# Starting the second expert layer on the first ten strips' rows while the last strips are still being routed

## The chip, the core and the metric

The kernel runs on one core of a Trainium2 chip. The metric is the device time of one execution in microseconds (us); for the kernel before, three runs were timed. A profile of one further execution on the same chip type gives the durations used below. Engines are TensorE (PE, with its weight loads as PEld), VectorE (DVE), ScalarE (ACT), GpSimd (POOL) and SyncE (SP); SP issues most of the plain loads and stores, GpSimd the indirect ones.

## What is computed

Two layers, each with a token mixer (windowed attention in layer 0, two ternary 3x3 convolutions with batch norm in layer 1) and a mixture of experts with 8 experts, of which each token uses 2. There are 2 x 56 x 56 = 6272 tokens of 256 channels. The part that the change touches is the experts of layer 1:

```python
def _L1_ffn_ref(x, gate_w, gate_b, W1, b1, W2, b2):
    ...
    logits = xf @ gate_w + gate_b
    probs = jax.nn.softmax(logits, axis=-1)
    top2_vals, top2_idx = jax.lax.top_k(probs, 2)
    cw = jnp.zeros((N, Ee), dtype=xf.dtype).at[jnp.arange(N)[:, None], top2_idx].add(top2_vals)

    def step(acc, params):
        w1, bb1, w2, bb2, we = params
        h = jax.nn.gelu(xf @ w1 + bb1, approximate=False)
        y = h @ w2 + bb2
        return (acc + we[:, None] * y, None)
...
x = x + _L1_conv_ref(_ln_c(x), ...)
t = _to_tokens(x)
t = t + _L1_ffn_ref(_ln_t(t), ...)
```

The hidden width of an expert is 512 in layer 1 and 256 in layer 0. The kernel computes only the two chosen experts of each token.

## The kernel before

**Tiling.** The image is cut into 14 strips of 8 rows, 448 tokens each, and a strip into 4 blocks of 112 tokens (`TT`). Experts work on tiles of `G` = 256 rows of one expert. Whatever the router says, `NTILE` = 56 tiles hold all 12544 token-expert pairs.

**Routing layer 1** (`routing`, L724, driven by `in_order`, L1816). For each strip, `residual` (L1783) loads the strip's tokens as they were ahead of the convolutions (`back`, two buffers, L1789, on SP's queue), finishes the batch norm and adds both (L1792, L1795, L1804, L1808). `norm` (L743) makes the normalised rows `u` (six buffers) and the logits (L758 to L781). `in_order` interleaves strips: a strip is begun in one turn of its loop, and its addition L1808 comes a turn later. `settle` (L786) takes a batch of strips (`BATCHES`, the last ones in pairs), finds the two best experts of each token and the row of each pair in its expert's part of the array `xs` in HBM. Then it issues, on GpSimd's queue, one indirect DMA for each block and choice that scatters 112 rows to `xs` (L854): 8 for a strip, 112 in all. The row's place depends on the tokens ahead of it, so that places grow from strip to strip.

**Planning.** After all strips, `tiles(1)` (L885) computes on VectorE, from the counts of rows of each expert, which expert and which first row each tile has (`where`), and `gates` (L867) the weights of the sums. `tiles` can also be called for a part: `tiles(0)` plans those tiles that are certain to be full after the first `FIRST[layer]` strips, and `tiles(1, taken)` the others. Layer 0 does this with `FIRST[0]` = 10 and so `EARLY[0]` = 27 early tiles. Layer 1 has `FIRST[1]` = 0, so that all 56 tiles are planned at the end and read their rows after all scatters.

**Experts** (`experts`, L982, and `experts_in_order`, L988). The order is written out by hand. For each tile, `fetch_weights` (L1012) reads the expert's number into a register of SP and loads 1.15 MB of weights (four buffers, three tiles ahead); `fetch_rows` (L999) reads the first row and loads 256 rows (six buffers, four ahead). `turn` (L1019) transposes the rows on TensorE and copies them on ScalarE (L1025, L1029), `first` (L1047) is the first product with its gelu (L1056, L1063), and `second` (L1065) the second product, the bias on VectorE (L1080, five buffers of y) and two scatters to `ys` on GpSimd's queue (L1082).

**Order.** `manual_schedule` keeps the order of the Python text on SP, VectorE, TensorE and ScalarE. All instructions of an engine, and the loads of SP's queue, are issued in that order, and an instruction that waits holds up those behind it. Dependencies between DMAs that touch the same array are taken as real unless two groups are declared apart: `disjoint` (L633) and `apart` (L639). Pools are stacks in SBUF: a pool that is opened where another was closed waits for that one's users.

**The last stage** (L1859 on) gathers each token's two rows from `ys`, adds them with the gates' weights, and writes the output.

Of the kernel before, what the change touches and what calls it, by code (L numbers as in the profile page):

```python
# [13 lines left out]
I32 = mybir.dt.int32  # L14
# [3 lines left out]
PSUM = bass.MemoryType.PSUM  # L18
# [42 lines left out]
TAPS = 9  # L61
COMPS = 4
DEN = HEADS * NT // TT
FIRST = (10, 0)

EARLY = tuple(max(0, (TOP * NT * n - E * (G - 1)) // G) for n in FIRST)
ROWS_AHEAD, AHEAD = 4, 3
# [559 lines left out]
def metaformer(ctx: ExitStack, tc: tile.TileContext, a: dict, out: bass.AP, flag):  # L627
# [354 lines left out]
    def experts(layer, FF, plans, ys, wp, tp, ps, at_tile=None):  # L982


        with tc.manual_schedule(engines=ENGINES):
            experts_in_order(layer, FF, plans, ys, wp, tp, ps, at_tile)

    def experts_in_order(layer, FF, plans, ys, wp, tp, ps, at_tile):  # L988
        NF = FF // P
        GP = G // P  # L990
        wts = a[f"L{layer}_experts"]
# [7 lines left out]
        def fetch_rows(j):  # L999
            where, _, _, n = planned(j)  # L1000
            r = nc.sync.value_load(
                where[0:1, 1, n : n + 1], min_val=0, max_val=E * ROWS - G
            )
            xg = tp.tile([P, GP, RW], F32, tag="xg", name="xg", bufs=6)
            o = nc.sync.dma_start(
                xg, xs[bass.ds(r, G), :].rearrange("(p i) c -> p i c", i=GP)
            )
            if j < EARLY[layer]:
                disjoint(o, f"early{layer}", f"late{layer}")
            live.setdefault(j, {})["xg"] = xg  # L1010

        def fetch_weights(j):  # L1012
# [79 lines left out]
        for j in range(AHEAD):  # L1092
            live[j] = {}
            fetch_weights(j)
        for j in range(ROWS_AHEAD):
            fetch_rows(j)
        turn(0)
# [2 lines left out]
        for j in range(NTILE):  # L1100
            if j + ROWS_AHEAD < NTILE:
                fetch_rows(j + ROWS_AHEAD)
            if j + AHEAD < NTILE:
                fetch_weights(j + AHEAD)
            if j + 2 < NTILE:
                turn(j + 2)
            if j + 1 < NTILE:
                first(j + 1)
            second(j)
            if at_tile is not None:  # L1110
                at_tile(j)

    def gather(i, ys, wgt, tp, xt, bufs):

# [140 lines left out]
    with ExitStack() as st:  # L1255
# [322 lines left out]
        x_all = None  # L1578
        X, XT, pad, sums = {}, {}, [], []
        mid = ctx.enter_context(ExitStack())  # L1580
        wq_held = ExitStack()

        def routed_all():

            nonlocal x_all
            plans0.append(tiles0(1, *taken))
            gates0()
            unfit = aw.tile([TT, 1], F32, tag="unfit", name="unfit")
            nc.vector.tensor_scalar(fits, fits, float(len(STRIPS)), None, ALU.is_lt)
            nc.vector.tensor_reduce(unfit, fits, AX.X, ALU.add)  # L1590
            unfit_b = aw.tile([TT, 1], BF16, tag="unfit_b", name="unfit_b")
            nc.vector.tensor_copy(unfit_b, unfit)
            pf = ps.tile([P, 1], F32, tag="aux", name="pf")
# [12 lines left out]
            cp = mid.enter_context(tc.tile_pool(name="pads", bufs=1, reuse_waits="tile"))  # L1606
            for b in range(B):
                t = cp.tile([P, KC, HC, WC], F32, tag=f"pad{b}", name=f"pad{b}")
                nc.gpsimd.memset(t[:, :, 0:1, :], 0.0)
                nc.gpsimd.memset(t[:, :, HC - 1 : HC, :], 0.0)  # L1610
                nc.gpsimd.memset(t[:, :, 1 : HC - 1, 0:1], 0.0)
                nc.gpsimd.memset(t[:, :, 1 : HC - 1, WC - 1 : WC], 0.0)
                pad.append(t)
            mid.enter_context(wq_held)
            wqp = wq_held.enter_context(tc.tile_pool(name="wq", bufs=1, reuse_waits="tile"))

            some = x_all[:, len(STRIPS) - 3 :].rearrange("p s c -> p (s c)").bitcast(BF16)
            sums.append(some.rearrange("p (k n c) -> p k n c", k=KC, n=COMPS))
            sums.append(wqp.tile([P, KC, COMPS, 3 * C], BF16, tag="sums", name="sums"))
# [23 lines left out]
    with mid:  # L1643
# [130 lines left out]
            scale2, shift2 = affine(stats, bn["g2"], bn["b2"], rt)  # L1774
        wq_held.close()

        wp1 = mid.enter_context(tc.tile_pool(name="moe_w1", bufs=4, reuse_waits="tile"))
        with ExitStack() as st:
            wp = st.enter_context(tc.tile_pool(name="route_w1", bufs=1, reuse_waits="tile"))
            tp = st.enter_context(tc.tile_pool(name="route_t1", bufs=2, reuse_waits="tile"))  # L1780
            ps = st.enter_context(tc.tile_pool(name="route_ps1", bufs=2, space=PSUM, reuse_waits="tile"))

            def residual(i):  # L1783

# [26 lines left out]
                yield from residual(i)  # L1811
                yield from norm(i, XT[STRIPS[i]][:TT])

            norm, settle, tiles, gates, wgt1, _ = routing(1, wp, tp, ps)

            def in_order():  # L1816

# [4 lines left out]
                for i in range(n + 2):  # L1822
                    young, old = i - 1, i - 2
                    if young in jobs:
                        next(jobs[young])
                    finish(ready)
                    if young == 0:
                        next(jobs[young])
                    if i < n:
                        jobs[i] = strip(i)  # L1830
                        next(jobs[i])
                    if young > 0 and young in jobs:
                        next(jobs[young])
# [155 lines left out]
```

## Time and profile before

| what | value |
|---|---|
| time, median of 3 runs | 1845.31 us (1836.94 to 1851.86) |
| profiled execution, its own time | 1841.35 us |
| its span, first to last instruction | 1839.5 us |
| TensorE busy | 1560.3 us, 85% |
| VectorE, ScalarE, GpSimd busy | 51%, 39%, 37% |
| routing of layer 1, about | 1178 to 1323 us |
| experts of layer 1, about | 1356 to 1770 us |
| gathering and output | the last 69 us |

Times within the profile count from the span's start. On a row of the timeline the first number is the start, the second how long it took (or, where rows were merged, x3 for example, from the first start to the last end), then engine, line, operation, and what is written from what, with the shape. In square brackets is how long the engine stood idle ahead of it and what ended the wait. The `SPq` rows are the issuing of DMAs on SP's queue, not their transfer.

### The profile page before, as it was taken

What the parts mean: (1) busy time and instruction counts of PE and PEld (TensorE: products, weight loads), DVE (VectorE), ACT (ScalarE), POOL (GpSimd) and SP (SyncE); (2) the same over time, 40 slices, a digit from 0 to 9 for tenths busy, and PEclk for the clock granted to TensorE, in tenths of its full rate; (3) what the DMA queues carried; (4) which work ended last, traced back from release to release, by engine and by line L of the source; (5) the groups of instructions that cost most, each with busy time, mean ns of one, the idle gap of its engine ahead of it and who ended that gap; (6) DMA issues with size and microseconds to landing.
All of it is one profiled execution on the core that took longest, in us unless ns stands there. A gap on an engine that the chain in (4) does not pass through costs nothing. (4 is left out here: it accounts for less than half of the span.)

```text
span 1839.5 us, 25711 instructions
## 1 busy us (share of the span) xinstructions
PE 1560.3 (85%) x8649; PEld 1233.4 (67%) x8649; DVE 934.5 (51%) x2618; ACT 709.1 (39%) x1347; POOL 677.6 (37%) x682
## 2 busy tenths in 40 slices
PE   6999997998768969866889899788359999999964
PEld 3555564555457857754778788677348888888852
DVE  3457657465625367847886555587501111111137
ACT  3454443343323434536553622255223333333312
POOL 3012544424423764442454143067732222222210
PEclk9999999999878989987999899855569999999975
DMA  8022333212257977866441000044446666666648
GB/s 246 21 83 83 112 101 114 72 45 80 83 159 228 302 276 247 303 208 194 145 144 31 0 1 1 21 121 134 164 141 229 237 237 225 228 234 234 216 150 308
DMA packets 89742, 283.23 MB, mean 154 GB/s; under 512 B 20391, under 2 KB 32763, under 8 KB 79297
## 3 DMA queue, kind: packets, MB, share of 16 engines
q1 hardware_dynamic: 64288, 223.25, 38.3%
q0 software_dynamic: 21504, 51.82, 8.0%
q10 hardware_dynamic: 3808, 6.42, 1.0%
q8 instruction: 70, 1.15, 0.3%
q14 instruction: 72, 0.58, 0.1%
HBM read 209.98 MB, written 75.12 MB: 155 GB/s over the span
## 5 line engine op out<-in xcount | busy, mean ns | idle before, releaser
L1056 PE MATMUL ph<-ut,w 128*128 128x256 f32 x1344 | 322.6, 391 | 5.5 <-DMA w<-in_L_experts 5.3
L1072 PE MATMUL py<-w,h 128*128 128x256 f32 x1344 | 310.3, 381 | 0.0
L1082 POOL DMA_INDIRECT ys<-y,to x170 | 170.7, 1004 | 370.9 <-DVE dest L1032 282.6
L1080 DVE TENSOR_TENSOR y<-py,w 128x512 f32<-128x512 f32 x112 | 77.4, 691 | 436.0 <-PE py L1072 318.9
L1072 PEld LDWEIGHTS py<-w,h 128*128 128x128 f32 x1344 | 257.7, 192 | 36.0
L1056 PEld LDWEIGHTS ph<-ut,w 128*128 128x128 f32 x1344 | 255.5, 197 | 39.1 <-DMA w<-in_L_experts 6.9
L1714 PE MATMUL pc<-hi,wq 128*128 128x448 f32 x672 | 256.8, 383 | 17.8 <-ACT hi L1685 17.8
L854 POOL DMA_INDIRECT xs<-u,pos x224 | 217.4, 971 | 127.7 <-issue 61.6
L1714 PE MATMUL pc<-lo,wq 128*128 128x448 f32 x672 | 255.8, 381 | 0.0
L1063 ACT ACTIVATE h<-ph,w 128x256 f32<-128x256 f32 x336 | 158.2, 474 | 123.7 <-PE ph L1056 123.2
L1416 ACT ACTIVATE ex<-sc 112x476 f32<-112x476 f32 (+3 forms) x224 | 116.3, 571 | 208.9 <-PE sc L1406 207.9
L1029 ACT COPY ut<-pt 128x512 f32<-128x512 f32 x112 | 65.5, 585 | 313.5 <-PE pt L1025 313.5
L1684 POOL TENSOR_TENSOR v<-pad 128x928 f32<-128x928 f32 (+1 forms) x56 | 98.3, 1762 | 162.6 <-DVE lo L1686 152.6
L1714 PEld LDWEIGHTS pc<-hi,wq 128*128 128x128 f32 x672 | 129.5, 193 | 33.1 <-ACT hi L1685 19.1
L1714 PEld LDWEIGHTS pc<-lo,wq 128*128 128x128 f32 x672 | 129.9, 193 | 15.1 <-DVE lo L1686 0.7
L1426 PE MATMUL av<-ex,vals 112*64 112x238 f32 (+3 forms) x896 | 121.2, 391 | 19.0 <-DVE acc L1436 18.8
L1025 PE MATMUL pt<-ident,xg 128*128 128x128 f32 x448 | 71.3, 284 | 60.6 <-DMA xg<-xs 57.7
L1436 DVE TENSOR_TENSOR acc<-av,acc 128x238 f32<-128x238 f32 (+3 forms) x224 | 87.3, 407 | 66.1 <-PE av L1426 64.0
L1025 PEld LDWEIGHTS pt<-ident,xg 128*128 128x128 f32 x448 | 57.6, 147 | 85.0 <-DMA xg<-xs 58.5
L1426 PEld LDWEIGHTS av<-ex,vals 112*64 112x64 f32 x896 | 55.6, 139 | 66.8 <-DVE acc L1436 24.8
L1685 ACT CAST hi<-v 128x928 fp32r<-128x928 f32 x56 | 54.1, 966 | 114.0 <-PE pc L1714 107.2
L1397 PE MATMUL sc<-q_im,keys 32*112 32x238 f32 (+3 forms) x896 | 89.7, 418 | 2.0 <-ACT ex L1416 1.9
(233 smaller groups left out, 2206.5 us busy)
## 6 DMA issues: line engine op xcount, KB each, us to landing
w<-in_L_experts SPq DMA_DIRECT2D x56, 1154.0 KB
w<-in_L_experts SPq DMA_DIRECT2D x56, 641.0 KB
xg<-xs SPq DMA_DIRECT2D x112, 260.0 KB
got<-ys SPq DMA_DIRECT2D x28, 896.0 KB
acc<-in_fresh SPq DMA_DIRECT2D x14, 896.0 KB
xt<-in_x_tok SPq DMA_DIRECT2D x14, 448.0 KB
xr<-in_x_tok SPq DMA_DIRECT2D x14, 448.0 KB
rec<-shares SPq DMA_DIRECT2D x28, 224.0 KB
```

What stands on the lines that cost most here:

```text
L854: w = nc.gpsimd.indirect_dma_start(xs[:, :], bass.IndirectOffsetOnAxis(ap=pos[:, j, t0 + t : t0 + t + 1], axis=0), us[t // NTT][:, t % NTT ...
L1025: nc.tensor.transpose(pt[:, k, i * P : (i + 1) * P], d["xg"][:, i, k * P : (k + 1) * P], ident)
L1056: nc.tensor.matmul(ph[:, :G], w1[:, k, f * P : (f + 1) * P], d["ut"][:, k, :], start=k == 0, stop=k == KC - 1,)
L1063: nc.scalar.activation(d["h"][:, f, :], ph[:, :G], AF.Gelu, bias=b1[:, f : f + 1])
L1072: nc.tensor.matmul(py[:, i, :], d["h"][:, f, i * P : (i + 1) * P], w2[:, f, :], start=f == 0, stop=f == NF - 1,)
L1082: o = nc.gpsimd.indirect_dma_start(ys[:, :], bass.IndirectOffsetOnAxis(ap=d["to"][:, i : i + 1], axis=0), y[:, i, :], None, bounds_check=T ...
L1397: nc.tensor.matmul(sc[h // 2][:, h % 2, :nq], keys[g][p, c, tx * TT : (tx + 1) * TT], q_im[p, c, r0:r1, c0:c1], start=True, stop=False,)
L1416: nc.scalar.activation(e[:, :, :nq], sc[j][:, :, :nq], AF.Exp, scale=HD**-0.5)
L1426: nc.tensor.matmul(av[VW * i : VW * (i + 1), :nq], vals[g % 3][:, tx, 2 * c + j, 2 * i : 2 * i + 2, :].rearrange("p a d -> p (a d)"), ex[j ...
L1436: nc.vector.tensor_tensor(d, av[:, :nq].rearrange("p (h w) -> p h w", w=c1 - c0), d, ALU.add)
L1684: (nc.gpsimd if u else nc.vector).tensor_tensor(v[:, :, at : at + n, :], *r, op)
L1714: nc.tensor.matmul(pc[:, :NT], wq[:, k, c, dx * C + o * P : dx * C + (o + 1) * P], part[:, k, :, dx : dx + W], start=m == 0, stop=m == 2 * ...
```

## The change

Layer 1 now also plans in two parts: 27 tiles from the first ten strips, the other 29 at the end. The experts' driver becomes a generator in three steps. The first step, which loads the weights of the first three tiles, is run inside the routing loop, as soon as strip 9 has been settled (which is in the turn that begins strip 12, ahead of that strip's first instructions). A load of one element of `xs` on GpSimd's queue (`fence`) follows there. After planning and gates, SP reads the loaded element, and then the experts go on; their early tiles' row loads are declared apart from all of layer 1's scatters. The pools for weights and routing move to the right side of SBUF, and the pads of the convolution are closed when routing is over, so that the tiles' buffers can be opened there.

```diff
-FIRST = (10, 0)
+FIRST = (10, 10)
...
         with tc.manual_schedule(engines=ENGINES):
-            experts_in_order(layer, FF, plans, ys, wp, tp, ps, at_tile)
-
-    def experts_in_order(layer, FF, plans, ys, wp, tp, ps, at_tile):
+            steps = experts_in_order(layer, FF, plans, ys, wp, at_tile)
+            next(steps)
+            steps.send((tp, ps))
+
+    def experts_in_order(layer, FF, plans, ys, wp, at_tile):
...
             if j < EARLY[layer]:
-                disjoint(o, f"early{layer}", f"late{layer}")
+                disjoint(o, f"early{layer}", f"rows{layer}" if layer else f"late{layer}")
...
         for j in range(AHEAD):
             live[j] = {}
             fetch_weights(j)
+        tp, ps = yield
         for j in range(ROWS_AHEAD):
             fetch_rows(j)
...
+        yield
...
-            cp = mid.enter_context(tc.tile_pool(name="pads", bufs=1, reuse_waits="tile"))
+            cp = pads.enter_context(tc.tile_pool(name="pads", bufs=1, reuse_waits="tile"))
...
-        wp1 = mid.enter_context(tc.tile_pool(name="moe_w1", bufs=4, reuse_waits="tile"))
-        with ExitStack() as st:
-            wp = st.enter_context(tc.tile_pool(name="route_w1", bufs=1, reuse_waits="tile"))
-            tp = st.enter_context(tc.tile_pool(name="route_t1", bufs=2, reuse_waits="tile"))
-            ps = st.enter_context(tc.tile_pool(name="route_ps1", bufs=2, space=PSUM, reuse_waits="tile"))
+        with ExitStack() as both:
+            wp1 = both.enter_context(
+                tc.tile_pool(name="moe_w1", bufs=4, side="right", reuse_waits="tile")
+            )
...
-            norm, settle, tiles, gates, wgt1, _ = routing(1, wp, tp, ps)
+            norm, settle, tiles, gates, wgt1, sent = routing(1, wp, tp, ps)
+
+            def fence():
+
+                some = wp.tile([1, 1], I32, tag="some", name="some")
+                nc.gpsimd.dma_start(some, xs[0:1, 0:1].bitcast(I32))
+                fences.append(some)
...
                     finish(ready)
+                    if not plans1 and FIRST[1] - 1 in sent:
+                        plan, n_early = tiles(0)
+                        plans1.append(plan)
+                        next(experts1)
+                        fence()
                     if young == 0:
...
                 finish(ready)
-
+                return n_early
+
+            plans1, fences = [], []
+            experts1 = experts_in_order(1, 2 * C, plans1, ys[1], wp1, None)
             with tc.manual_schedule(engines=ENGINES):
-                in_order()
-                plans1 = [None, tiles(1)]
+                plans1.append(tiles(1, in_order()))
                 gates()
 
-        with ExitStack() as st:
-            tp = st.enter_context(tc.tile_pool(name="moe_t1", bufs=2, reuse_waits="tile"))
-            ps = st.enter_context(tc.tile_pool(name="moe_ps1", bufs=2, space=PSUM, reuse_waits="tile"))
-            experts(1, 2 * C, plans1, ys[1], wp1, tp, ps)
+                nc.sync.value_load(fences[0])
+
+                route_ps.close()
+                pads.close()
+                tp1 = both.enter_context(tc.tile_pool(name="moe_t1", bufs=2, reuse_waits="tile"))
+                ps1 = both.enter_context(
+                    tc.tile_pool(name="moe_ps1", bufs=2, space=PSUM, reuse_waits="tile")
+                )
+                experts1.send((tp1, ps1))
```

`side="right"` stands on `route_w1` and `route_t1` as well.

More of the change, by code (lines that the diff above doesn't have):

```diff
@@ L1580, in metaformer @@
         mid = ctx.enter_context(ExitStack())
+        pads = mid.enter_context(ExitStack())
         wq_held = ExitStack()
@@ L1775, in metaformer @@
         wq_held.close()
-        wp1 = mid.enter_context(tc.tile_pool(name="moe_w1", bufs=4, reuse_waits="tile"))
-        with ExitStack() as st:
-            wp = st.enter_context(tc.tile_pool(name="route_w1", bufs=1, reuse_waits="tile"))
-            tp = st.enter_context(tc.tile_pool(name="route_t1", bufs=2, reuse_waits="tile"))
-            ps = st.enter_context(tc.tile_pool(name="route_ps1", bufs=2, space=PSUM, reuse_waits="tile"))
+        with ExitStack() as both:
+            wp1 = both.enter_context(
+                tc.tile_pool(name="moe_w1", bufs=4, side="right", reuse_waits="tile")
+            )
+            wp = both.enter_context(
+                tc.tile_pool(name="route_w1", bufs=1, side="right", reuse_waits="tile")
+            )
+            tp = both.enter_context(
+                tc.tile_pool(name="route_t1", bufs=2, side="right", reuse_waits="tile")
+            )
+            route_ps = ExitStack()
+            ps = route_ps.enter_context(
+                tc.tile_pool(name="route_ps1", bufs=2, space=PSUM, reuse_waits="tile")
+            )
             def residual(i):
@@ L1847, in in_order @@
                 finish(ready)
+                return n_early
+            plans1, fences = [], []
+            experts1 = experts_in_order(1, 2 * C, plans1, ys[1], wp1, None)
             with tc.manual_schedule(engines=ENGINES):
-                in_order()
-                plans1 = [None, tiles(1)]
+                plans1.append(tiles(1, in_order()))
                 gates()
-        with ExitStack() as st:
-            tp = st.enter_context(tc.tile_pool(name="moe_t1", bufs=2, reuse_waits="tile"))
-            ps = st.enter_context(tc.tile_pool(name="moe_ps1", bufs=2, space=PSUM, reuse_waits="tile"))
-            experts(1, 2 * C, plans1, ys[1], wp1, tp, ps)
+                nc.sync.value_load(fences[0])
[4 more added lines that the diff above has]
+                    tc.tile_pool(name="moe_ps1", bufs=2, space=PSUM, reuse_waits="tile")
+                )
+                experts1.send((tp1, ps1))
     with ExitStack() as st:
```

## The prediction

> **What bounds the kernel now.** I looked first at the forty slices: TensorE falls to 3 and then 5 tenths in slices 28 and 29, between the second convolution and the last long run of nines, and the granted clock is 5 tenths there. The chain of waits, read in order of time, has that place as scatters of layer 1 (L854), then a row load, then expert matmuls back to back. The timeline shows why.
>
> ```profile
> 1312.81 0.17 DVE L847 CAST pos<-rowf 112x16 int32<-112x16 f32 x1
> ...
> 1319.03 0.17 DVE L949 CAST where<-ex 1x56 int32<-1x56 f32 x1
> ...
> 1320.51 2.62 SPq L1016 DMA_DIRECT2D w<-in_L_experts  x3
> ...
> 1322.11 0.28 ACT L875 ACTIVATE wgt<-wgt 112x112 f32<-112x112 f32 x1
> ...
> 1350.52 0.94 POOL L854 DMA_INDIRECT xs<-u,pos  x1 [0.30 <-issue]
> 1353.21 5.05 SPq L1005 DMA_DIRECT2D xg<-xs  x5
> ...
> 1355.93 1.11 PE L1025 MATMUL pt<-ident,xg 128*128 128x128 f32 x4 [42.62 <-DMA xg<-xs]
> ...
> 1357.08 0.59 ACT L1029 COPY ut<-pt 128x512 f32<-128x512 f32 x1 [34.69 <-PE pt L1025]
> ...
> 1358.35 5.28 PE L1056 MATMUL ph<-ut,w 128*128 128x256 f32 x16
> ```
>
> The last strips' places are known at 1312.98 and the plan and gates are done by 1322.39 (ScalarE's second exponential), but GpSimd, with one 112-row scatter each 1.246 us (0.94 and 0.30 idle), ends 1351.46. The first row load waits for all of them. TensorE stands 42.62 us, and from 1358 to 1770 it is busy 413.6 of 414 us in the table of windows. So each microsecond by which the first L1056 starts earlier comes off the end, as long as the tiles stay fed. Without the rows' wait, ScalarE could copy the first transposed tile from 1322.39. Its copy began 1.06 us before L1056's weight load (1357.08 to 1358.14), so that load could start at 1323.45: **34.7 us** at most are to be had.
>
> What the change puts into routing falls into the stretch where strip 12 starts:
>
> ```profile
> 1282.54 2.78 PE L772 MATMUL pl<-gate,ut 128*112 128x8 f32 x14 [0.42 <-ACT ut L763]
> 1282.78 0.17 DVE L847 CAST pos<-rowf 112x16 int32<-112x16 f32 x1
> 1282.86 1.27 DVE L1792 SCALAR_TENSOR_TENSOR x<-x,scale,pad 128x448 f32<-128x448 f32 x2
> ...
> 1287.20 1.23 DVE L1808 TENSOR_TENSOR x<-pt,back 112x1024 f32<-112x1024 f32 x1 [1.65 <-PE pt L1804]
> ```
>
> The first is strip 10's router product, the second places strips 8 and 9, the third and fourth are strip 12's two residual steps; the fourth needs its `back` rows. VectorE is busy 90.8 of 110 us from 1190 to 1300, so work put in here moves the end of routing.
>
> [...] five `got` loads of about 0.92 MB each were issued from 1775.11 within 2.70 us, and the first was used at 1781.17, when about 1.38 MB had moved (ten half-microsecond slices); loads served in equal shares would not have finished one so early. [...] scatters alone move 93 GB/s, with the three weight loads the total is 400 to 440 GB/s. [...] here the first sixteen L1056 took 5.07 us against 3.46 later. The change starts from an idle TensorE too, so I count that at nothing.
>
> **The change part by part.**
>
> *Rows before the last strips (the gain).* Tiles 0 to 26 wait for a one-element read (`fence`) behind strip 9's scatters instead of for the last one. 32 scatters come after it, so it is issued near 1351.46 - 32 x 1.246 = 1311.6. It waits for the scatter ahead (2.6 us median to landing) and lands itself; no such small GpSimd load is in the trace[...]. I take 3: rows may be read from 1317, five row loads need 5.05 us, the first is in by 1320. That is before routing ends, so the fence costs the start nothing, up to some 15 us of lateness.
>
> *The fence on GpSimd's queue.* The next scatter waits for it, some 5.6 us. Behind it are 32 xs scatters, which then end near 1357.5, or up to 3 us later if strip 10's places are late too. No early tile waits for them. The first output scatter stood at 1371.98, 12.9 us after the first y's tile began; it moves to about 1355 and waits 3 to 5 us, against five y buffers of 7.35 us each. Tile 27 reads rows some 23 tiles later. Nothing.
>
> *tiles(0) on VectorE (a loss).* Layer 0 runs the same function with the same 27 columns:
>
> ```profile
> 511.94 0.13 DVE L907 TENSOR_SCALAR cnt<-counts 128x8 f32<-128x8 f32 x1
> ...
> 514.47 0.16 DVE L949 CAST where<-ex 1x27 int32<-1x27 f32 x1
> ...
> 515.65 0.17 DVE L954 CAST where<-first 1x27 int32<-1x27 f32 x1
> 515.73 0.36 SPq L1016 DMA_DIRECT2D w<-in_L_experts  x1
> ```
>
> In the built order the `counts` product stands behind all of strip 10's router products, which end at 1285.32. So VectorE stands from 1282.95 to about 1285.6, then needs 3.7 us to L954 and some 0.7 for L956 to L959: L1792 of strip 12 goes from 1282.86 to 1290.1, **7.2 us** late, all on the path.
>
> *Three weight loads ahead of strip 12's `back` (a loss).* SP issues in order: the three loads wait for L949 (near 1285.6 + 2.5 = 1288.1, and 1.26 to 1.48 us more to the issue: 1289.5); `back` 12, until now issued at 1271.33, comes fourth. In the trace the same three loads moved from 1323.0 to 1334.0 beside scatters, their end 13.5 us after the first issue at 1320.51: 3.46 MB at 310 GB/s. `back` adds 0.46 MB, 1.5 us[...]. It lands near 1305.0. L1808 of strip 12 would start at 1290.1 + 4.3 (today's distance, 1287.20 - 1282.86) = 1294.4. **10.6 us** of stall; `back` 13 follows closely, no second one. Behind the waiting L1808 are the settling of strips 10 and 11 and all of strip 13; they are chains of VectorE, ScalarE and TensorE steps and GpSimd has a backlog of scatters, so I let nothing be caught up.
>
> *Planning of the late tiles.* With 29 columns and the subtraction of what is taken, layer 0 needed 7.79 us from L905 to L872 (654.09 to 661.88), layer 1 with 56 columns 7.63 (1313.35 to 1320.98): **+0.2**. One more copy of `seen`, 0.2, lies in that rounding.
>
> *Pools.* Weights and routing pools move to the other side of SBUF and the tiles' buffers onto the pads. Their earlier users are layer 0's experts, and the pads' early rows, long done. The gate's load, now issued at 1177.94, can go earlier; its first reader is at 1192.81. Nothing; 1 us either way. Number of tiles, matmuls and weight loads stay: 56 each. In the first 16 us GpSimd's scatters (93 GB/s) lie beside the tiles' mean 218 GB/s; 311 is below the 400 seen. Nothing, up to 3 us lost.
>
> Sum: -34.7 + 7.2 + 10.6 + 0.2 = -16.7. The first L1056 weight load goes from 1358.1 to 1341.4 and the profiled span from 1839.5 to 1822.8, its time from 1841.35 to 1824.6. That execution lay 4 us below the median of 1845.31, inside the three runs; from the median: **1828.6**.
>
> **The rivals.**
>
> *A. `back` isn't held up.* The engines give it a share beside the weights, or the weights move faster. For it: only 0.46 MB. Against: the in-order `got` loads. Without the stall, -34.7 + 7.4 = -27.3: 1818.
>
> *B. Rows still wait for the last scatter.* If the declared independence doesn't hold, the first row load follows the last scatter, which the fence has moved by 5.6 us: 1845.3 + 5.6 = 1851, slower than before. Against: in the built order the first row loads carry the fence's wait only.
>
> *C. The weights starve routing.* [...] The gain is used up when `back` lands 16.7 us after 1305, that is with the three weights at 3.46 MB / (11.2 + 16.7) = 124 GB/s; at 100 GB/s it gives 1852, and 1% slower needs some 74 GB/s. The trace's 310 beside scatters speaks against it.
>
> **How the numbers follow.** My forecast 0.60 (1822 to 1836 with the bounds above and 4 us of run noise), A 0.25 (1812 to 1824), B 0.08, C 0.07. One per cent, about what a measurement of this kernel tells from no change, is 18.5 us: below 1826.9. My forecast's centre is just short of that, with some four in ten of it beyond: 0.24; with nearly all of A, faster is 0.47. The rest of the forecast, B and half of C: 0.47 within 1%. Slower by over 1%: 0.06. The range of 1813 to 1843 leaves out B, C and the edge of A.
>
> **What would show it.** Right: in the changed profile a wait of VectorE at strip 12's residual addition for a DMA of about 10 us, the weight loads near 1290 and `back` 12 after them; a row load landing near 1320; the last xs scatters beside the first tiles; first L1056 near 1341, then tiles at 7.35 us without gaps. Wrong: no such wait (A), row loads after the last scatter (B), a wait of 25 us or more (C), or gaps between the first tiles for w or for y buffers.

## The result and the profile after

The changed kernel took 1824.48 us (median of 12 runs, 1820.01 to 1839.03), the kernel before, run beside it, 1845.55 us (12 runs): a ratio of 0.9908 over all runs, 95% interval 0.9888 to 0.9929. That is 17 us less (13 to 21); the medians alone lie 21 us apart. The profiled execution took 1821.12 us, its span is 1819.0 against 1839.5.

From the experts on, the lines of the changed file stand 3 to 15 further down: L1807 and L1823 are now the two residual steps, L1019 the weight loads, L1008 the row loads, L1028 and L1032 the transposes and their copy, L1059 the first product, L1085 the scatters to `ys`. The timeline of the kernel after, from the moment at which strips 8 and 9 are placed (first line, VectorE L847):

```profile
1273.69 0.24 DVE L847 CAST pos<-rowf 112x16 int32<-112x16 f32 x1
...
1276.10 0.17 DVE L907 TENSOR_SCALAR cnt<-counts 128x8 f32<-128x8 f32 x1 [2.18 <-PE counts L898]
...
1280.67 1.27 DVE L1807 SCALAR_TENSOR_TENSOR x<-x,scale,pad 128x448 f32<-128x448 f32 x2
1280.91 3.39 SPq L1019 DMA_DIRECT2D w<-in_L_experts  x3
1284.41 1.12 SPq L1804 DMA_DIRECT2D back<-x_mid  x2
...
1298.32 1.22 DVE L1823 TENSOR_TENSOR x<-pt,back 112x1024 f32<-112x1024 f32 x1 [15.56 <-DMA back<-x_mid]
1303.10 0.60 POOL L1834 DMA_DIRECT2D some<-xs  x1 [2.27 <-DMA xs<-u,pos]
1305.61 4.83 SPq L1008 DMA_DIRECT2D xg<-xs  x5
1311.92 0.98 POOL L854 DMA_INDIRECT xs<-u,pos  x1 [8.22 <-DVE u L751]
...
1332.06 0.62 DVE L872 TENSOR_TENSOR lgs<-lgs,most 112x448 f32<-112x448 f32 x1
...
1333.20 0.28 ACT L875 ACTIVATE wgt<-wgt 112x112 f32<-112x112 f32 x1
...
1334.00 6.02 PE L1059 MATMUL ph<-ut,w 128*128 128x256 f32 x16 [7.83 <-ACT ut L1032]
...
1351.25 0.94 POOL L854 DMA_INDIRECT xs<-u,pos  x1 [0.30 <-issue]
1352.50 1.01 POOL L1085 DMA_INDIRECT ys<-y,dest  x1 [0.30 <-issue]
```

Read it against the lines of before. The row loads (1305.61) now stand ahead of 32 scatters instead of behind them, and the last scatter to `xs` (1351.25) runs beside the tiles. In exchange VectorE waits 15.56 us for `back`, which stands behind the three weight loads on SP, and the first product no longer waits for rows: it waits for ScalarE's copy, and that for the exponential at 1333.20 and, through L872, for VectorE's planning.

The two executions differ upstream too: the places of strips 8 and 9 come at 1273.69 here, at 1282.78 before. Most of these 9.1 us is there when layer 0's last scatter is issued (656.73 against 665.42), and two more profiles of kernels with the change, on the fourth chip below, have the places at 1282.25 and 1279.97. So I take it as the spread of executions and count from that place; that none of it comes from the moved pools is not shown. The first expert product came 75.6 us after it before (1358.35), and comes 60.3 us after it now. From there to the end the span needs 485.0 us, before 481.15. Thus the two spans differ by 9.1 (upstream) + 15.3 (here) - 3.8 (later) = 20.5 us, up to rounding.

### The profile page after: what moved, and what is told of

It reads as the page before. It is cut to its first block, busy times and chain, and to the rows that moved or that the text cites. A ratio compares the mean times of both kernels' runs of the same rounds, so it can differ in the third digit from the quotient of the medians.

```text
span 1819.0 us, 25693 instructions
## 1 busy us (share of the span) xinstructions
PE 1556.4 (86%) x8650; PEld 1230.8 (68%) x8650; DVE 925.4 (51%) x2590; ACT 708.4 (39%) x1347; POOL 678.9 (37%) x683
## 3 DMA queue, kind: packets, MB, share of 16 engines
q8 instruction: 70, 1.15, 0.3%
## 4 chain that ended last, share of the span: by engine, by line
PE 39%; DVE 7%; DMA 7%; issue 5%; ACT 3%; POOL 2%; SPq 0%; POOLq 0%; DVEq 0%; ACTq 0%
PE ph L1059 12%; PE py L1075 12%; PE pc L1720 12%; DMA out<-o_out 2%; DMA got<-ys 2%; PE pt L1028 2%; DMA x_on<-x_mid 2%; POOL ys L1085 1%; DVE x_on L1139 1%; PE pl L772 1%; DVE t_stats L695 1%; PE pu L1150 1%; DMA back<-x_mid 1%; POOL x_on L1143 1%; ACT xn L716 1%
## 5 line engine op out<-in xcount | busy, mean ns | idle before, releaser
L1059 PE MATMUL ph<-ut,w 128*128 128x256 f32 x1344 | 317.8, 388 | 13.8 <-ACT ut L1032 7.8
L1059 PEld LDWEIGHTS ph<-ut,w 128*128 128x128 f32 x1344 | 253.0, 195 | 46.3 <-ACT ut L1032 8.2
L1720 PE MATMUL pc<-hi,wq 128*128 128x448 f32 x672 | 256.7, 383 | 16.6 <-ACT hi L1691 16.6
L854 POOL DMA_INDIRECT xs<-u,pos x224 | 218.1, 974 | 136.0 <-issue 61.0
L1085 POOL DMA_INDIRECT ys<-y,to x116 | 118.8, 1024 | 208.8 <-DVE dest L1035 135.6
L1085 POOL DMA_INDIRECT ys<-y,dest x108 | 108.0, 1000 | 195.1 <-DVE dest L1035 141.0
L1032 ACT COPY ut<-pt 128x512 f32<-128x512 f32 x112 | 65.3, 584 | 279.0 <-PE pt L1028 278.9
L1720 PEld LDWEIGHTS pc<-hi,wq 128*128 128x128 f32 x672 | 129.6, 193 | 31.6 <-ACT hi L1691 18.0
L1431 PEld LDWEIGHTS av<-ex,vals 112*64 112x64 f32 x896 | 56.3, 141 | 62.0 <-issue 26.5
L1028 PE MATMUL pt<-ident,xg 128*128 128x128 f32 x448 | 70.1, 281 | 20.0 <-DMA xg<-xs 14.3
```

Source lines behind the costliest of these rows:

```text
L854: w = nc.gpsimd.indirect_dma_start(xs[:, :], bass.IndirectOffsetOnAxis(ap=pos[:, j, t0 + t : t0 + t + 1], axis=0), us[t // NTT][:, t % NTT ...
L1028: nc.tensor.transpose(pt[:, k, i * P : (i + 1) * P], d["xg"][:, i, k * P : (k + 1) * P], ident)
L1059: nc.tensor.matmul(ph[:, :G], w1[:, k, f * P : (f + 1) * P], d["ut"][:, k, :], start=k == 0, stop=k == KC - 1,)
L1085: o = nc.gpsimd.indirect_dma_start(ys[:, :], bass.IndirectOffsetOnAxis(ap=d["to"][:, i : i + 1], axis=0), y[:, i, :], None, bounds_check=T ...
L1431: nc.tensor.matmul(av[VW * i : VW * (i + 1), :nq], vals[g % 3][:, tx, 2 * c + j, 2 * i : 2 * i + 2, :].rearrange("p a d -> p (a d)"), ex[j ...
L1720: nc.tensor.matmul(pc[:, :NT], wq[:, k, c, dx * C + o * P : dx * C + (o + 1) * P], part[:, k, :, dx : dx + W], start=m == 0, stop=m == 2 * ...
```

## Experiments

They ran on four chips, called second to fifth (the fourth may be the first again; that isn't recorded). They fall into two kinds: on the fourth the kernel before takes 1845.36 us, as on the first; on the second, third and fifth it takes 1957.04, 1969.05 and 1966.1. Times are compared within a chip only. "Places" and "product" are the distances, in us, from the places of strips 8 and 9 to those of 12 and 13 and to the first expert product, each from one profile.

| kernel | chip | time, us (runs) | ratio to before, 95% interval | places | product |
|---|---|---|---|---|---|
| before | first | 1845.55 (12) | | 30.0 | 75.6 |
| changed | first | 1824.48 (12) | 0.9908 (0.9888 to 0.9929) | 50.2 | 60.3 |
| before | second | 1957.04 (13) | | 40.3 | 77.8 |
| changed | second | 1962.19 (1) | | 54.9 | 88.8 |
| weights later | second | 1962.79 (7) | 1.0025 (1.0003 to 1.0046) | 47.8 | 81.8 |
| rows wait | second | 1969.53 (7) | 1.0054 (1.0027 to 1.008) | 55.1 | 89.8 |
| changed | third | 1973.06 (7) | 1.0046 (1.0023 to 1.007) | 56.1 | 90.9 |
| exponentials first | third | 1972.69 (5) | 1.0026 (1.0004 to 1.0048) | 56.3 | 64.5 |
| back first | third | 1958.27 (20) | 0.9954 (0.9931 to 0.9977) | 51.1 | 63.5 |
| both | third | 1950.39 (4) | 0.991 (0.9888 to 0.9931) | 52.5 | 55.7 |
| hold scatters | fourth | 1829.53 (1) | | 49.7 | 59.9 |
| both | fourth | 1809.42 (4) | 0.9808 (0.9777 to 0.9838) | 29.8 | 43.6 |
| weights later | fifth | 1964.07 (20) | 0.999 (0.9969 to 1.0011) | 50.3 | 82.3 |
| hold scatters | fifth | 1970.15 (1) | | 55.2 | 88.0 |

**The two kernels on the second chip.**

> The kernel before, unchanged, profiled once more. In the two profiles at hand the places of strips 8 and 9 (VectorE's L847) were ready at 1282.8 us before and at 1273.7 us after the change, though nothing ahead of them was edited but pools and the order of two small loads. If that is the spread of executions, this point lies anywhere between some 1272 and 1285 here, and the distance from it to the first expert product stays 75.6 us within 1 us. If the change itself made it earlier, it lies at 1281 or later.

> The changed kernel, unchanged, profiled once more. Distance from the places of strips 8 and 9 to the first expert product 60.3 us within 1 us, with a wait of VectorE of 14 to 17 us at strip 12's residual addition. From the first expert product to the end of the span 485.0 us was measured, against 481.2 us before the change: if the last stage's loads are slower by the change, 484 to 486 again; if that was the spread of executions, it may be 481.

This was the surprise: the change gained nothing there, and the distances expected of the first chip, 75.6 and 60.3 us, came out at 77.8 and 88.8. The places of strips 8 and 9 lie 2.5 us apart (1387.35 and 1384.85), and from the first product to the end the changed kernel needs 486.3 us against 483.5: again some 3 us more. In the waits views of the stretch from 1250 to 1480 us, the kernel before:

```profile
PE pt L1025 <- DMA xg<-xs: 35.0, 2, 34.3
...
DVE x L1808 <- remote: 13.0, 2, 7.4
```

and the changed kernel on the same chip:

```profile
ACT lgs L873 <- DVE lgs L872: 39.4, 1, 39.4
...
PE ph L1059 <- ACT ut L1032: 31.6, 1, 31.6
...
DVE x L1823 <- DMA back<-x_mid: 18.4, 1, 18.4
```

The columns are microseconds in all, how often, the longest. The wait of 34.3 us for rows is gone as on the first chip, and one of 31.6 us for ScalarE's copy stands in its place, against 7.83 on the first. ScalarE stood 39.4 us for L872, the end of VectorE's planning. ("remote" is a wait whose releaser the profile doesn't know.)

**Undoing one part each.** The weights of the first three tiles behind the routing in the order of the text ("weights later" in the table):

```diff
-                        next(experts1)
                         fence()
...
-                plans1.append(tiles(1, in_order()))
+                n_early = in_order()
+                next(experts1)
+                plans1.append(tiles(1, n_early))
```

On SP's queue this puts them behind both `back`, and no later than that: their first issue comes 10.7 us after the places of strips 8 and 9 (1404.81), as in the changed kernel (1395.58).

> The three weight loads come after strip 13's back rows on SP's queue instead of ahead of strip 12's. My theory (the back rows stood behind the weights in the queue): the wait at strip 12's residual addition is gone, so the routing ends 13 us earlier; first expert product 47 us after the places of strips 8 and 9 instead of 60.3; time 1811 us, 0.7% below the changed kernel. Rival (the wait is hidden by GpSimd's backlog or by another wait behind it, such as the fence): first expert product stays at 55 us or later and the time within 4 us of 1824.

and the early tiles' rows waiting for all scatters again ("rows wait"):

```diff
-            if j < EARLY[layer]:
-                disjoint(o, f"early{layer}", f"rows{layer}" if layer else f"late{layer}")
+            if j < EARLY[layer] and layer == 0:
+                disjoint(o, f"early{layer}", f"late{layer}")
```

> As the changed kernel, but the early tiles' row loads wait for all of layer 1's scatters. My theory (the gain is the row loads' freedom from the last scatters): the first expert product follows the last scatter by 6.9 us as before, the last scatter ends 79.4 us after the places of strips 8 and 9 because of the fence and the late routing, so the first product comes at 86 us, 10.7 us later than before the change; time 1856 us. Rival (the gain comes from elsewhere, such as the pools or the split plan): time stays within 6 us of 1824.

Strip 12's residual steps in the timeline of the changed kernel on the second chip:

```profile
1393.70 1.28 DVE L1807 SCALAR_TENSOR_TENSOR x<-x,scale,pad 128x448 f32<-128x448 f32 x2
1414.20 1.22 DVE L1823 TENSOR_TENSOR x<-pt,back 112x1024 f32<-112x1024 f32 x1 [18.43 <-DMA back<-x_mid]
```

and with the weights behind `back`:

```profile
1402.93 1.27 DVE L1807 SCALAR_TENSOR_TENSOR x<-x,scale,pad 128x448 f32<-128x448 f32 x2
1406.80 1.23 DVE L1823 TENSOR_TENSOR x<-pt,back 112x1024 f32<-112x1024 f32 x1 [1.80 <-ACT u L716]
```

Between the two steps lie 20.5 us with the weights ahead of `back` and 3.9 with them behind: the weights ahead of `back` make the stall, as the prediction had it. The places of strips 12 and 13 come 7.1 us earlier, and so does the product (88.8 to 81.8); the rest of the 16.6 us was made up by other waits. The time shows no difference against the changed kernel's single run. On this chip the expected 47 us for the product was far off, since VectorE's planning, not the places alone, set it.

With the rows waiting, the time against before is what was expected (1.0054; 10.7 us would be 1.0055), but not for the whole reason: the product at 89.8 is only 1.1 us later than in the changed kernel. So reading the rows ahead of the last scatters is worth about 1 us here, where the planning ends just as late. On a chip as the first this edit was not run; what the rows are worth there is read from its profiles alone.

The first edit ran again on the fifth chip:

> The first weights loaded after the routing again, with the early planning and the rows left where the change has them. Theory, on a chip that doesn't stretch the routing (the chip of the profile after and that of the run with 0.981): VectorE's 13 us wait for back goes, the places of strips 12 and 13 come about 37 us after those of 8 and 9 instead of 50, the first expert product at 47 instead of 60, and the time is 9 to 13 us below the changed kernel's (0.984 to 0.986 of the kernel before). Rival: the weights, issued 10 us later or more, hold the first product instead, and the ratio stays at 0.990 or above. On a chip that stretches it: 1.0025 as before.

Product at 82.3, against 88.0 for the changed kernel but for one scatter (below); ratio 0.999. Again no gain to speak of. On a chip as the first this edit was not run either, so that the 9 to 13 us expected there are not shown.

**What follows the rows.** If VectorE's late planning now sets the product, releasing ScalarE's exponentials ahead of it must bring the product forward:

```diff
-            nc.scalar.activation(wgt, wgt, AF.Exp)
+            nc.scalar.activation(wgt, wgt, AF.Exp); yield
...
-                plans1.append(tiles(1, in_order()))
-                gates()
+                n_early = in_order(); weigh = gates(); next(weigh)
+                plans1.append(tiles(1, n_early)); finish(weigh)
```

Of VectorE's instructions, only L872 and L874 change their place against the planning. In the next kernel the early planning and the three weight loads move, besides, behind the start of strip 12, so that one `back` is issued ahead of them:

```diff
-                    if not plans1 and FIRST[1] - 1 in sent:
-                        plan, n_early = tiles(0)
-                        plans1.append(plan)
-                        next(experts1)
+                    if not fences and FIRST[1] - 1 in sent:
                         fence()
...
                         jobs[i] = strip(i)
                         next(jobs[i])
+                    if fences and not plans1:
+                        plan, n_early = tiles(0)
+                        plans1.append(plan); next(experts1)
```

and in the third ("both") they move behind strip 12's logits, a turn later, so that both `back` are ahead:

```diff
                     if old == 0:
                         finish(steps)
+                    if young == n - 1:
+                        plan, n_early = tiles(0)
+                        plans1.append(plan)
+                        next(experts1)
                     if young in jobs:
                         next(jobs[young])
```

The four ran together on the third chip.

> The changed kernel again, timed, as the measure for the three edits beside it on the same chip. Theory 1 (what sets the first expert product differs with the chip): where VectorE's late planning takes about 7.7 us, as in the profile after, the ratio to before is near 0.991 and the first expert product comes about 60 us after the places of strips 8 and 9; where that planning takes about 31 us, as in the profiles of the second chip, the ratio is 1.00 to 1.006 and the product comes at about 89 us. Theory 2 (the gain was an accident of one set of runs): the ratio goes with neither.

> The two subtractions that release ScalarE's two exponentials go ahead of the planning of the late tiles; nothing else moves on any engine. Theory: ScalarE's copy of the first tile's transposed rows stands behind the exponentials, and so behind the late planning on VectorE; with the edit the first expert product comes about 6 us earlier where the planning takes 7.7 us (about 54 us after the places of strips 8 and 9, time 6 us less than the changed kernel), and about 27 us earlier where it takes 31 us (of which 8 to 10 come back as a stall of TensorE two tiles later, since VectorE still has to finish the planning before it can take the products out: 17 to 19 us less). Rival: the rows or the first weights land late anyway, and the time stays within 1 us of the changed kernel.

> As the run before, and the early planning with its three weight loads goes behind the issue of strip 12's back and behind strip 12's first two VectorE operations, the pause on GpSimd stays where it is. Theory: the 13 to 18 us for which VectorE waits for back 12 go; the places of strips 12 and 13 come 34 to 37 us after those of 8 and 9 instead of 50 (first chip), and the first expert product at 40 to 46 instead of 60: 14 to 20 us less than the changed kernel on a chip as the first, 25 to 30 on one as the second. Rival: the wait for back moves to strip 13, whose back still stands behind the three weight loads, and 10 us or more of it stay; or the rows aren't there before 50.

> As the run with the exponentials released first, and the early planning with its three weight loads goes to strip 13's turn, behind strip 12's logits; both backs are then issued ahead of the weights. Theory: no wait for back at all, strips 12 and 13 placed 33 to 35 us after 8 and 9, but the weights are issued some 20 us later than in the changed kernel, land about 17 us after their issue, and the first expert product waits for them until 44 to 48 us: 12 to 16 us less than the changed kernel on a chip as the first. Rival: weights and rows share the DMA engines and the product comes at 55 or later: 5 us or less.

The changed kernel's late planning in its timeline on the third chip, from its first instruction (L905) to L872, which follows it:

```profile
1446.95 0.17 DVE L905 COPY cnt<-counts 128x8 f32<-128x8 f32 x1 [0.28 <-PE counts L898]
...
1463.79 0.37 DVE L943 TENSOR_REDUCE first<-past 128x29 f32<-128x203 f32 x1 [2.28 <-issue]
1465.19 0.19 DVE L944 TENSOR_TENSOR first<-tabs,first 128x29 f32<-128x29 f32 x1 [1.03 <-issue]
1466.59 0.19 DVE L946 TENSOR_TENSOR first<-first,at 128x29 f32<-128x29 f32 x1 [1.21 <-issue]
...
1472.89 0.19 DVE L966 TENSOR_TENSOR last<-first,last 128x29 f32<-128x29 f32 x1 [4.48 <-remote]
...
1479.34 0.62 DVE L872 TENSOR_TENSOR lgs<-lgs,most 112x448 f32<-112x448 f32 x1
```

and the same on the first chip:

```profile
1324.40 0.17 DVE L905 COPY cnt<-counts 128x8 f32<-128x8 f32 x1 [0.29 <-PE counts L898]
...
1329.49 0.37 DVE L943 TENSOR_REDUCE first<-past 128x29 f32<-128x203 f32 x1
1329.89 0.19 DVE L944 TENSOR_TENSOR first<-tabs,first 128x29 f32<-128x29 f32 x1
1330.12 0.19 DVE L946 TENSOR_TENSOR first<-first,at 128x29 f32<-128x29 f32 x1
```

The instructions themselves take the same 0.37 and 0.19 us, but start 1.40 us apart instead of 0.40 and 0.23, with longer holes between. L905 to L872 is 32.4 us there, 31.3 on the second chip, 7.66 on the first. These 24.7 us more and the places of strips 12 and 13, 5.9 us later (56.1 against 50.2), make up the 30.6 us by which the product comes later than on the first chip.

Exponentials first: the product comes 26.4 us earlier, as expected (27). But TensorE and ScalarE then stand still themselves, as this kernel's timeline on the third chip has it:

```profile
1459.91 5.39 PE L1059 MATMUL ph<-ut,w 128*128 128x256 f32 x16 [5.19 <-issue]
...
1468.42 0.59 ACT L1032 COPY ut<-pt 128x512 f32<-128x512 f32 x1 [8.56 <-issue]
...
1480.13 2.07 PE L1059 MATMUL ph<-ut,w 128*128 128x256 f32 x4 [14.39 <-issue]
```

"issue" is a wait for nothing that the profile shows. From the third tile on (its first product at 1494.39, 98.9 us after the places; changed kernel 1494.01, 103.7) the tiles run without gaps, and 4.7 us of the lead are left. The time is 1972.69 against 1973.06: no difference clear of the noise, where 17 to 19 us were expected. I had expected 8 to 10 us to come back, as a stall for VectorE's sake; 21.7 did, most of it in waits that the profile can't name. So the planning did set the product, but it is not by itself what costs the time on this chip: once it is out of the way, TensorE and ScalarE meet such waits themselves.

Back first gains 15 us against the changed kernel (25 to 30 expected), both edits gain 23. Each holds the exponentials' edit as well, which alone gained nothing here. VectorE's wait for `back` is 3.24 us, at strip 13, in the former, and none in the latter, where 8.27 us with an unknown releaser stand ahead of strip 13's addition instead.

**Scatters as the cause?** The stretched planning always lay beside GpSimd's scatters. This kernel was to hold the last 16 of them until the planning is done:

```diff
+            if layer and strips[-1] == len(STRIPS) - 1:
+                sent.append(send(strips, us, t0, n, rowf))
+                return
...
+                some = wp.tile([1, 1], I32, tag="done", name="done")
+                nc.gpsimd.tensor_copy(some, plans1[1][1][0:1, 0, 0:1]); finish(sent[-1])
```

> The changed kernel, with the 16 scatters of strips 12 and 13 held on GpSimd until VectorE has finished the planning of the late tiles (a one-element copy of its last output stands ahead of them); the result is the same. Theory: on the second and third chip the late planning takes 31 to 33 us instead of 7.7 [...] so with no scatter beside it the planning ends some 8 us after the scatters of strips 10 and 11 and takes 8 to 16 us, the first expert product comes about 70 us after the places of strips 8 and 9 instead of 89 to 91, and stalls show up beside the first tiles instead, where the held scatters now run. Rival: it takes about 30 us again with GpSimd idle, and the cause lies elsewhere. On a chip as the first, where the planning is not stretched, both expect the product at 60 us as before.

> The same kernel as the run that held the scatters, for the case that this chip stretches the late planning. Theory (scatters starve the other engines there): the planning ends within 8 to 16 us of its start, once the scatters of strips 10 and 11 are through. Rival: it takes about 30 us with GpSimd idle. On a chip that doesn't stretch it, 7.7 us and the first product at 60 us, as before.

It does not do so: GpSimd is not among the engines whose order the hand-written schedule keeps, and 15 of the 16 were still issued ahead of the copy. The timeline on the fifth chip, around the end of the planning:

```profile
1475.43 0.94 POOL L860 DMA_INDIRECT xs<-u,pos  x1 [0.30 <-issue]
...
1480.11 0.17 DVE L976 CAST where<-first 1x29 int32<-1x29 f32 x1 [2.61 <-remote]
...
1481.81 0.51 POOL L1887 COPY done<-held 1x1 int32<-1x1 int32 x1 [5.44 <-DVE held L983]
...
1482.48 0.96 POOL L860 DMA_INDIRECT xs<-u,pos  x1 [0.17 <-issue]
```

So both runs are the changed kernel but for one scatter, and serve as its profile on the fourth and fifth chip: the product at 59.9 and at 88.0 us. Whether the scatters stretch the planning is open: GpSimd stood idle for the last 5.4 us of it, and VectorE still waited 2.61 us with an unknown releaser, but the last scatter ahead of that wait was issued at 1475.43, and in the profile of before on the first chip a scatter takes 2.6 to 7.0 us from issue to landing, so that rows may still have been on their way.

**Both edits again**, on the fourth chip:

> The best version so far (exponentials released before the late planning; early planning and its weights in strip 13's turn), timed again. Theory: about 0.991 of the kernel before on a chip as the second or third; on a chip as the first 0.978 to 0.985, since nothing there stretches the planning and the first expert product comes at 44 to 48 us after the places of strips 8 and 9 instead of 60 in the changed kernel. Rival: on a chip as the first it gives no more than the changed kernel's 0.991, because weights and rows then land late.

0.9808 (0.9777 to 0.9838), inside the 0.978 to 0.985 expected: the fastest version, ahead of both kernels on the third chip and on the fourth. Its timeline there, in which the places of strips 8 and 9 stand at 1279.97:

```profile
1304.39 2.77 SPq L1019 DMA_DIRECT2D w<-in_L_experts  x3
...
1309.88 0.62 DVE L872 TENSOR_TENSOR lgs<-lgs,most 112x448 f32<-112x448 f32 x1
...
1311.02 0.28 ACT L875 ACTIVATE wgt<-wgt 112x112 f32<-112x112 f32 x1
...
1314.13 0.60 POOL L1834 DMA_DIRECT2D some<-xs  x1 [6.68 <-DMA xs<-u,pos]
...
1317.92 5.27 SPq L1008 DMA_DIRECT2D xg<-xs  x5
...
1321.84 0.59 ACT L1032 COPY ut<-pt 128x512 f32<-128x512 f32 x1 [10.54 <-PE pt L1028]
...
1323.57 5.77 PE L1059 MATMUL ph<-ut,w 128*128 128x256 f32 x16
```

The exponentials are done at 1311.3, and the copy waits for the transposed rows, whose loads wait for the `fence`: with the other two waits gone, the rows set the start again. Here, on a chip of the first kind, the stall is undone too: the places of strips 12 and 13 come after 29.8 us, before the change after 30.0, and VectorE doesn't wait for `back`. What each of the two moves gives by itself on such a chip was not run.

## Why the prediction was right, and how far

It said 1828.6 us and 1813 to 1843; measured were 1824.48. Step by step, from the profiles of the first chip, counted from the places of strips 8 and 9:

- **Rows before the last strips.** Rows to be read 34.2 us after the places (the prediction's 1317), measured 31.9 (1305.61): the `fence` is issued at 29.4, its wait of 2.27 us for the scatter ahead included, and SP goes on 2.5 us later; the 3 us that the prediction took for it to land were an estimate of mine, shown by no trace. It cost the start nothing.
- **The fence on GpSimd's queue.** The pause before the next scatter is longer than the 5.6 us given (8.22 us idle after the fence), since GpSimd then waits for strip 10's places; that lateness was named. The first scatter to `ys` follows the last to `xs` at once, and no tile waits.
- **tiles(0) on VectorE.** Predicted 7.2 us late, measured 6.9: strip 12's L1807 starts 6.98 us after the places instead of 0.08.
- **Weights ahead of `back`.** Predicted stall 10.6, measured 13.3 us (L1823 at 1298.32 instead of 1280.67 + 4.34, the distance of before). Here a size was off: from the first weight issue to the use of `back` it took 17.4 us, where the terms were 13.5 for the weights, 1.5 for `back` and 0.5 more, an allowance of mine that no trace shows. What carried this step is the order in which the prediction's five `got` loads came in (the first used when 1.38 MB had moved), and the runs agree: with the weights behind `back`, the distance between the two steps falls from 20.5 to 3.9 us on the second chip.
- **No catching up.** From strips 10 and 11 to 12 and 13 the places need 12.92 us, as before.
- **Planning of the late tiles.** Predicted +0.2, measured +0.03 (7.66 against 7.63).
- **Sum.** Predicted -16.7, measured 75.6 to 60.3, -15.3. With the measured losses the sum would be -34.7 + 6.9 + 13.3 = -14.5; the other 0.8 is that the copy no longer follows the second exponential at a distance (1333.38, 0.1 us ahead of its end) and the first product comes 0.5 us after it, where the bound had 1.06 to the weight load and 0.2 from there to the product.
- **After the first product.** Some 3.8 us are lost there, where the prediction allowed up to 3 us for slow loads beside the first tiles and nothing further on. Most of it is in the last stage: from TensorE's last expert product to the end 71.9 us instead of 68.8, with VectorE's waits for gathered rows a little longer at several strips. In the other profiles of the changed kernel (one scatter aside) this stage takes 72.1 to 74.5 us, in the second of the kernel before 70.6. Why is not known.

So the mechanism held step by step, but the closeness of the total is in part luck. The steps give 15.3 - 3.8 = 11.5 us, less than the 13 to 21 us of the ratio's interval. The 5.5 us up to its 17 were not in the prediction's sum. In the two profiles the missing part stands upstream, where the executions differ by 9.1 us; whether the change has a share in that is open.

Of the rivals, A (`back` not held up) and B (rows wait for the last scatter) are excluded by the two lines at 1298.32 and 1305.61. C, weights so slow that they use up the gain, did not come either: 3.46 MB of weights and 0.46 MB of `back` in 17.4 us are some 225 GB/s, less than the 310 that I took and more than the 124 at which the gain is gone. It isn't what takes the gain on the second and third chip: first weight issue to the use of `back` is 18.6 us there, hardly more than on the first.

What the prediction did not see is the mechanism by which it would have been wrong on another chip. It made the first product hang on VectorE's planning, and took the length of that from one chip. In the kernel before, the planning was stretched on the second chip as well (22.6 us from the second counts product to ScalarE's second exponential, L875, against 9.0 on the first), but lay under the wait for rows. There the step "Planning of the late tiles, +0.2" would have had to be some +24, which with the stalls of the routing ends above before. And even that step isn't all: with the exponentials first, the planning is off the path, and the time is still that of the changed kernel.

## What to carry to other kernels

Taking away the last wait hands the path to what was hidden under it: ask what that is, and what it costs if it runs slower than in the one profile at hand; here 7.7 us of small VectorE instructions became 32. And look at the time as well as at the wait that is gone: one kernel brought its first product 26 us forward on the third chip and gained nothing. Load prefetches behind what the path needs next on the same queue (here VectorE waited 15.56 us for `back` behind them), and put work that only later steps need (plans for late tiles) behind what releases the first step. And make sure, before an order is part of an argument, that the engine in question keeps the order of the text (GpSimd issued 15 of 16 scatters ahead of the copy that was to hold them).

## What was not expected of the hardware

Chips differ in this program by 6 to 7% (1957.04 to 1969.05 us against 1845.36 and 1845.55 for the kernel before), and not evenly. The routing of layer 1, from strip 0's first batch-norm activation (1179.53 on the first, 1256.90 on the second chip) to the places of the last strips (1312.81 and 1427.62), took the kernel before 133 and 171 us, though the instructions compared take as long on both (medians: ScalarE's L1795 0.671 us, GpSimd's L854 0.942) and full tiles of layer 1 take 7.35 us on both. What grows are waits for nothing that the profile shows, on VectorE, ScalarE and TensorE, and with them the issue of the three weight loads, which contains SP's waits for the plan: 2.6 to 3.4 us on the first and fourth chip, 9.2 to 18.2 on the others. The mean granted TensorE clock is lower too (0.866 against 0.890 in the kernel before), but VectorE's instructions last as long on both kinds of chip (0.37 and 0.19 us above), and only the gaps between them grow. It isn't the amount of DMA traffic. The windows of the planning, first of the changed kernel on the second chip, with busy time of TensorE, its weight loads, VectorE, ScalarE and GpSimd, then the granted clock, the DMA share and GB/s:

```profile
1450.00:1455.00 5.00, 0.00 (x0) 0.00 (x0) 0.77 (x3) 0.00 (x0) 3.77 (x4) 0.50 0.31 93
```

and on the first:

```profile
1325.00:1330.00 5.00, 1.17 (x6) 0.77 (x4) 4.55 (x17) 0.00 (x0) 3.78 (x5) 0.50 0.27 83
```

Scatters, DMA share and clock are alike; VectorE ran 3 instructions in 5 us on the one, 17 on the other. VectorE's and ScalarE's waits with an unknown releaser, summed over the whole kernel before on the second chip, have a place: 26 of them with 161.8 us from 188 to 745 us, 10 with 62.7 us from 1255 to 1460, none elsewhere. Those are the stretches in which GpSimd scatters to `xs` (layer 0 from 188.70 to 736, layer 1 to 1456.2); the scatters to `ys`, which go on to the end of the experts, have none beside them. On the first chip the same kernel has none at all, nor do the two profiles on the fourth show one from 1200 to 1370 us. And in all ten profiles on the slower kind of chip, the last wait of 1 us or more for nothing that the profile knows, on TensorE (its weight loads left out), VectorE or ScalarE, ends at most 5.4 us after the last scatter to `xs`, whether planning or tiles run by then.

So the scatters to `xs` are the first suspect. But routing runs in these stretches as well, the kernel that was to hold the scatters didn't hold them, and no cause is shown. What the profile's two instruction queues moved is no difference either: in the kernel before, 70 packets with 1.15 MB on the one on both kinds of chip, and 72 (first chip) or 71 (second) with 0.58 MB on the other. Which of the two kinds of chip one gets decides what the change is worth: the ratio was 0.9908 on the first, 1.0046 on the third.
